# Cross-attention with a scan on one core: when x is loaded, when the scan's inputs are multiplied, and what durations the planner is given

## The chip, the cores and the metric

One core of a Trainium2 chip runs the whole kernel in one launch. The metric is device time in microseconds (us). The runs of the kernel before gave 2028.73, 2029.94 and 2029.88 us, a median of 2029.88 us.

## The reference

Everything is float32. T = 4096 tokens of width H = 512 attend with 8 heads of 64 to 3202 keys; a layer norm, a recurrent scan and an added row follow.

```python
residual = x
q_in, kv_in = layernorm(x, g1, beta1), layernorm(ctx, g1, beta1)
x = residual + mha(q_in, kv_in, W_qkv, b_qkv, W_o, b_o)      # softmax over 3202 keys
residual = x
U = (layernorm(x, g2, beta2) @ W_in.T + b_in) @ Bmat           # 64 numbers a token
s_t = silu(s_{t-1} @ A.T) + U_t                                # scan over 4096 tokens
x = residual + states @ Cmat
out = x + (ctxb.mean(axis=1) @ W_prog.T + b_prog)
```

## The kernel before

**Preparation** (the first 213 us): the context is normed, turned and multiplied into keys and values, which go to DRAM (kd, vd).

**Attention.** The 4096 tokens are eight query blocks Q of 512. A unit is one (Q, pair of heads hp, half of the block), 64 units in all, and a unit has 13 chunks of 256 keys. One chunk of one unit is a step; step number 13 x unit + chunk, 832 in all, and about 104 to a query block. A step is a matmul of scores (`scores`, s, L635), an exp on ScalarE (`weights`, p, L705), a matmul with the values four steps later (`product`, po, L745) and an addition for the softmax sum (`add`, acc, L713): VectorE does nine of a unit's twelve, GpSimd those of chunks 2, 6 and 10. At the end of a unit GpSimd folds the sum (`fold`, L720), TensorE sums it over partitions (`sums`, pd, L763), ScalarE reads it (`denominators`, L797), and VectorE adds, inverts and applies it (`whole` L801, `inverse` L804, `scale` L811, `fall` L807).

**Queries** (`queries`): while block Q is attended, x of block Q+1 is loaded in two halves of two tiles (L880), normed (`stats` L845 on VectorE, `factors` L849 to L851 on GpSimd, `scaled` xh, L857 on ScalarE), transposed in 32x32 blocks on VectorE (`flip`, L932), and moved between partitions by DMAs from SyncE's queue (`move`, L944: four pieces of four DMAs for each half). Four matmul pieces (`heads`, pq, L312) then make q. Block 7 is not flipped and moved but transposed on TensorE.

**Rows** (`project`): when block Q is done, while block Q+1 is attended, each half of its outputs is multiplied with W_o (`outs`, pa, L987, 7.1 us). x is loaded again (xr, L978), GpSimd adds a constant row (`row`, L981), VectorE adds the two (`x1`, L1000), GpSimd adds another row for the final output (`mod`, L1004), which is stored (L1007); the norm follows as for the queries, then `flip` (L932), four `move` pieces (16 DMAs, L944) and the matmul of the scan's inputs (`inputs`, pu, L1042), copied by `kept` (L1051). Tiles are named by their first token: pa_256 and pu_256 are the second half of block 0, xr_2816 the second half of block 5.

**Scan and end.** Two sweeps of 16 steps over 256 token groups follow; the last 256 tokens have a chain of their own (`last_rows`), which starts from yb (L1332).

**What sets the order.** No engine's order is written by hand. `Plan` holds pieces with an engine, a duration, the pieces they follow, a due time and rings of buffers they take and give; `order()` simulates the engines with these durations and emits the program in the order that comes out. Each engine and SyncE's queue then run in that order. A piece with the earliest due time among those ready goes first. On TensorE a piece that is not of the 64x64 kind pays 30000 ns (`ALONE`, 14 steps) on its due time unless another such piece is ready as well. `load_k` and `load_v` (L1098, L1106, ten and six steps ahead) are issued inside `scores`; the planner gives them no time on SyncE. A `move` piece is given 2600 ns there. Ring `x` has two buffers, shared by the queries' and the rows' loads; `x1` and `xn2` have one each. A due time is counted from d, the time at which a half's work begins; `from_(d)` makes a load follow a given step's scores.

Of the kernel before, what the change touches and what calls it, by code (L numbers as in the profile page):

```python
# [25 lines left out]
NDC = NCH // 2  # L26
# [22 lines left out]
STEP = 2150  # L49
# [121 lines left out]
def xattn_ssm_kernel(  # L171
# [349 lines left out]
    with tc.manual_schedule():  # L521
# [18 lines left out]
        first = shift(1)  # L540
        for c in range(NCH):
# [5 lines left out]
            parts = 1 if c < NCH - 1 else 2  # L547
            for i in range(NC // parts):
                for h in range(parts):
                    k = h * NC // parts + i  # L550
# [30 lines left out]
            for hp in range(NC):  # L581
# [9 lines left out]
                ks = cin.tile([P, GC * CK], F32, tag="ks", name=f"ks_{g}_{hp}")  # L591
# [3 lines left out]
                for b in range(g * GC, c + 1, 2):  # L595
                    m, k = blocks(b // 2) * CK, key0(b) - key0(g * GC)
# [189 lines left out]
    def finish(w, i, d, plan):  # L786

        name = w["name"]
        last = w["last"]
        ring = "s" if last else "m"  # L790

        def denominators(k):
            if k == 0:
                w["rd"] = op.tile([P, QU], F32, tag="rd", name=f"rd_{name}", bufs=2)
            of = rows_of(w, w["pd"][k][:, :QU], True)
            to = of if k else rows_of(w, w["rd"])
            nc.scalar.activation(to, of, AF.Copy, accum_out=rises[:, 3 * i + k : 3 * i + k + 1])  # L797

        def whole():
            rd = rows_of(w, w["rd"])  # L800
            nc.vector.tensor_tensor(rd, rows_of(w, w["pd"][1][:, :QU], True), rd, ALU.add)  # L801

        def inverse(part):
            nc.vector.reciprocal(w["rd"][:, part], w["rd"][:, part])  # L804

        def fall():
            nc.vector.tensor_reduce(rises[:, 3 * i + 2 : 3 * i + 3], w["rd"], AX.X, ALU.add)  # L807

        def scale(part):
            o = o_t[w["at"]][:, part]  # L810
            nc.vector.tensor_tensor(o, o, w["rd"][:, part], ALU.mult)  # L811

        plan.add(("output", i), "ACT", 360, partial(output, w), [("product", i, NDC - 1)], d, ["o_"])
        plan.add(("join", i), "DVE", 430, partial(join, w), [("output", i)], d + 500, [],
                 [("o", ("product", i, 0))])
        plan.add(("fold", i), "POOL", 1250, partial(fold, w), [("add", i, NDC - 1)], d + 500)
        plan.add(("sums", i), "PE", 450, partial(sums, w), [("fold", i)], d + 1000,
                 ["s"] if last else ["m", "m"], [("acc", ("add", i, 1))], "quarters")
        for k in range(2):
            plan.add(("den", i, k), "ACT", 420, partial(denominators, k), [("den", i, 0) if k else ("sums", i)], d + 2500 + k,  # L820
                     [] if k else ["rd"], [(ring, ("sums", i))])
        plan.add(("whole", i), "DVE", 430, whole, [("den", i, 1)], d + 3000, [], [(ring, ("sums", i))])
        parts = [slice(t * P, (t + 1) * P) for t in range(2)] if last else [slice(0, QU)]
        for t, part in enumerate(parts):
            plan.add(("inverse", i, t), "DVE", 950 if last else 1750, partial(inverse, part),
                     [("whole", i)], d + 5000 + t)
            plan.add(("scale", i, t), "DVE", 400, partial(scale, part),
                     [("inverse", i, t), ("join", i)], d + 5000 + t if last else d + 8000, [],
                     [("rd", ("den", i, 0))])
        plan.add(("fall", i), "DVE", 340, fall, [("inverse", i, t) for t in range(len(parts))],  # L830
                 d + 9000, [], [("rd", ("den", i, 0))])

    def from_(d):

        return ("scores", *divmod(min(int(d / STEP), len(steps) - 1), NDC))

    def norm_pieces(plan, ks, gets, d, after, names, gives):


        vs = [{}, {}]  # L840

        def stats_(v, get, name):
            for k, n in (("st", nc.vector.BN_STATS_DIM), ("mv", nc.vector.BN_AGGR_DIM), ("rstd", 1), ("nm", 1)):
                v[k] = ln.tile([P, n], F32, tag=f"{k}_2", name=f"{k}_{name}")
            nc.vector.bn_stats(v["st"], get())  # L845
            nc.vector.bn_aggr(v["mv"], v["st"])

        def factors_(v):
            nc.gpsimd.tensor_scalar(v["rstd"], v["mv"][:, 1:2], EPS, None, ALU.add)  # L849
            nc.gpsimd.tensor_tensor(v["rstd"], v["rstd"], neg_half, ALU.pow)  # L850
            nc.gpsimd.tensor_scalar(v["nm"], v["mv"][:, 0:1], v["rstd"], -1.0, ALU.mult, ALU.mult)  # L851

        def scaled_(v, get, t):
            if t == 0:
                for w, name in zip(vs, names):
                    w["xh"] = ln.tile([P, H], F32, tag="xh", name=f"xh_{name}")
            nc.scalar.activation(v["xh"], get(), AF.Identity, bias=v["nm"], scale=v["rstd"])  # L857

        for t, (k, v) in enumerate(zip(ks, vs)):
            plan.add((*k, "stats"), "DVE", 870, partial(stats_, v, gets[t], names[t]), [after[t]],  # L860
                     d + t, ["fs"])
            plan.add((*k, "factors"), "POOL", 1050, partial(factors_, v), [(*k, "stats")], d + 2000)
            plan.add((*k, "scaled"), "ACT", 800, partial(scaled_, v, gets[t], t),
                     [(*k, "factors")] + ([(*ks[0], "scaled")] if t else []), d + 3 * STEP + t,
                     [] if t else ["xh", "xh"], [("fs", (*k, "stats"))] + gives[t : t + 1])
        return vs

    def queries(plan, Q, d):

        copied, w = [], {}  # L870
        of_xn = ("query", Q, 0, "move0") if mixes(Q) else ("queries", Q, 0, "turn")
        for half in range(2):
            ks = [("query", Q, half * 2 + t) for t in range(2)]
            at = [Q * QB + half * QU + t * P for t in range(2)]
            k2, v = ("queries", Q, half), {}
# [5 lines left out]

            for t in range(2):
                plan.add((*ks[t], "load"), "SP", 800, partial(load, t),
                         [(*ks[0], "load")] if t else [from_(d - 2 * STEP)], d - 2 * STEP + t, [] if t else ["x"])
            free = ("x", (*ks[0], "load"))
            nv = norm_pieces(plan, ks, [lambda t=t, v=v: v["x"][:, t] for t in range(2)], d,
                             [(*k, "load") for k in ks], [f"x{r}" for r in at],
# [18 lines left out]
            after = [of_xn] if half else []  # L906
# [58 lines left out]
    def project(plan, Q, halves, d, index):  # L965

        for half in halves:
            ks = [("row", Q, half * 2 + t) for t in range(2)]
            at = [Q * QB + half * QU + t * P for t in range(2)]
            k2, vs, w = ("rows", Q, half), [{}, {}], {}  # L970
# [38 lines left out]
            units_ = [index[Q, c, half] for c in range(NC)]  # L1009
            for t in range(2):  # L1010
                plan.add((*ks[t], "load"), "SP", 800, partial(load, t),
                         [(*ks[0], "load")] if t else [from_(d - 4 * STEP)], d - 4 * STEP + t, [] if t else ["x"])
                plan.add((*ks[t], "row"), "POOL", 1300, partial(row, vs[t]), [(*ks[t], "load")], d - STEP)
            plan.add((*k2, "outs"), "PE", 7200, outs,
                     [("scale", i, 0) for i in units_] + [(*k, "row") for k in ks], d - now,
# [43 lines left out]
            if last:  # L1059
                plan.add((*k2, "turn"), "PE", 1050, turn, [(*k, "scaled") for k in ks], d + 5 * STEP - now,  # L1060
                         ["m", "m", "xn2"], [("xh", (*ks[0], "scaled"))])
                for t in range(2):
                    plan.add((*ks[t], "copy"), "ACT", 560, partial(copy, t),
                             [(*k2, "turn")] + ([(*ks[0], "copy")] if t else []), d + 6 * STEP + t, [],
                             [("m", (*k2, "turn"))])
                copied, xn2, after = [(*k, "copy") for k in ks], (*k2, "turn"), 7
            else:
                copied, xn2, after = [], (*ks[0], "move0"), 16

                def move_(a, w=w, at=at):  # L1070
                    if a == 0:
                        w["xn"] = xp_.tile([P, NC, QU], F32, tag="xn2", name=f"xn2_{at[0]}", bufs=1)
                    move(w["xn"], w["x1"], a)

                for t in range(2):
                    plan.add((*ks[t], "flip"), "DVE", 720, lambda t=t, w=w, nv=nv: flip(w["x1"], nv[t]["xh"], t),
                             [(*k, of) for k in ks for of in ("scaled", "mod")], d + 5 * STEP + t, [],
                             [("xh", (*ks[0], "scaled"))])
                for a in range(P // TB):
                    plan.add((*ks[0], f"move{a}"), "SP", 2600, partial(move_, a),  # L1080
                             [(*k, "flip") for k in ks] + ([xn2] if a else []), d + (6 + 2 * a) * STEP,
                             [] if a else ["xn2"], [("x1", (*k2, "outs"))])
                    copied.append((*ks[0], f"move{a}"))
# [392 lines left out]
    def unit(plan, i):  # L1476
# [19 lines left out]
        if half == 0:  # L1496
            d = max(s0 - REF, 0) * STEP
# [9 lines left out]
        for c in range(NDC):  # L1507
# [23 lines left out]
                         ["acc"] if c == 1 else [],  # L1531
                         [p] + ([("p", ("weights", i, 0))] if c == 1 else []))
            if c == 1:
                plan.add(("rest", i), "DVE", 700, partial(rest, w), [("add", i, 1), ("extra", first)],
                         d + 1300, [], [("extra", ("extra", first))])
        d += 2000
        finish(w, i, d - 40 * STEP if w["last"] else d, plan)
# [348 lines left out]
```

## Time and profile before

| what | value |
|---|---|
| runs, median | 2029.88 us |
| profiled execution, its own time | 2036.71 us |
| span of that execution | 2034.9 us |
| mean granted TensorE clock | 0.988 |
| TensorE matmul busy (PE) | 1967.0 us, 97% |
| VectorE (DVE) / ScalarE (ACT) / GpSimd (POOL) busy | 1210.8 / 1134.3 / 796.7 us |
| SyncE queue: moves (L944) | 416 DMAs of 32 KB |

The profile's engines are PE (matmul), PEld (weight load), DVE, ACT, POOL and SP (SyncE; its queue is SPq). Instructions issue in order on each engine, so an idle time in front of one is put down to what released it. Times inside a window are counted from the span's start.

### The profile page before, as it was taken

What the parts mean: (1) busy time and instruction counts of PE and PEld (TensorE: products, weight loads), DVE (VectorE), ACT (ScalarE), POOL (GpSimd) and SP (SyncE); (2) the same over time, 40 slices, a digit from 0 to 9 for tenths busy, and PEclk for the clock granted to TensorE, in tenths of its full rate; (3) what the DMA queues carried; (4) which work ended last, traced back from release to release, by engine and by line L of the source; (5) the groups of instructions that cost most, each with busy time, mean ns of one, the idle gap of its engine ahead of it and who ended that gap; (6) DMA issues with size and microseconds to landing.
All of it is one profiled execution on the core that took longest, in us unless ns stands there. A gap on an engine that the chain in (4) does not pass through costs nothing.

```text
span 2034.9 us, 66527 instructions
## 1 busy us (share of the span) xinstructions
PE 1967.0 (97%) x29070; PEld 1258.4 (62%) x29070; DVE 1210.8 (60%) x1533; ACT 1134.3 (56%) x1478; POOL 796.7 (39%) x631
## 2 busy tenths in 40 slices
PE   8999999999999999999999999999999999989996
PEld 4444566665666666666666566666666666655674
DVE  4321367566766666666656675677556655655585
ACT  2233566665656555555666665656565565654553
POOL 2111234345433453345334643345334533444324
PEclk9999999999999999999999999999999999999998
DMA  5632333223422343224322342233322322544475
GB/s 170 188 102 64 100 95 90 59 80 93 110 71 77 92 110 87 76 69 110 90 63 81 83 108 65 80 105 102 83 77 77 93 75 63 149 139 116 123 201 197
DMA packets 246935, 204.28 MB, mean 100 GB/s; under 512 B 80809, under 2 KB 220073, under 8 KB 246637
## 3 DMA queue, kind: packets, MB, share of 16 engines
q1 hardware_dynamic: 242088, 192.28, 33.4%
q10 hardware_dynamic: 4548, 7.67, 1.3%
q8 instruction: 231, 3.78, 0.8%
q14 instruction: 68, 0.55, 0.1%
HBM read 156.32 MB, written 29.88 MB: 92 GB/s over the span
## 4 chain that ended last, share of the span: by engine, by line
PE 70%; DVE 11%; POOL 9%; issue 3%; SPq 3%; ACT 2%; DMA 2%; DVEq 0%; POOLq 0%; ACTq 0%
PE s L635 24%; PE po L745 24%; DVE acc L713 7%; PE pq L312 5%; POOL acc L713 4%; PE pk L584 4%; PE pv L551 4%; PE pa L987 3%; SPq L944 2%; ACT p L705 1%; PE pd L763 1%; DVE rd L804 1%; DMA x<-in_x_dram 1%; POOL rstd_x L850 1%; DVE acc L699 1%
## 5 line engine op out<-in xcount | busy, mean ns | idle before, releaser
L705 ACT ACTIVATE p<-s,shifts 128x1024 f32<-128x1024 f32 (+1 forms) x832 | 889.1, 1080 | 528.5 <-PE s L635 517.4
L635 PE MATMUL s<-q,k 64*64 64x256 f32 x12800 | 839.8, 379 | 16.7 <-ACT p L705 15.6
L713 DVE TENSOR_TENSOR acc<-p,acc 128x1024 f32<-128x1024 f32 (+1 forms) x515 | 620.2, 1204 | 381.4 <-POOL acc L713 315.7
L745 PE MATMUL po<-p,v 64*64 64x256 f32 x12800 | 825.1, 378 | 0.0
L713 POOL TENSOR_TENSOR acc<-p,acc 128x1024 f32<-128x1024 f32 x189 | 446.7, 2363 | 765.4 <-DVE acc L713 419.6
L635 PEld LDWEIGHTS s<-q,k 64*64 64x64 f32 x12800 | 485.9, 134 | 248.1 <-ACT p L705 36.5
L745 PEld LDWEIGHTS po<-p,v 64*64 64x64 f32 x12800 | 491.4, 134 | 192.8 <-issue 6.1
L720 POOL TENSOR_TENSOR acc<-acc 128x512 f32<-128x512 f32 x64 | 102.1, 1595 | 141.1 <-DVE acc L713 141.1
L713 DVE TENSOR_TENSOR acc<-p,p 128x1024 f32<-128x1024 f32 x64 | 95.9, 1499 | 40.0 <-ACT p L705 34.3
L312 PE MATMUL pq<-xn,wq 128*128 128x512 f32 x256 | 118.3, 605 | 0.0
L804 DVE RECIPROCAL rd<-rd 128x256 f32<-128x256 f32 (+1 forms) x65 | 112.4, 1729 | 2.2
L987 PE MATMUL pa<-wo,o 128*128 128x512 f32 x240 | 107.0, 599 | 0.0
L551 PE MATMUL pv<-wv,ct 128*128 128x512 f32 (+1 forms) x208 | 96.4, 617 | 1.0 <-ACT ct L519 0.7
L584 PE MATMUL pk<-ct,wk 128*128 128x512 f32 (+1 forms) x224 | 88.8, 549 | 0.0
L784 DVE TENSOR_TENSOR o<-po,o 128x256 f32<-128x256 f32 x64 | 27.1, 423 | 95.3 <-ACT o L780 94.8
L312 PEld LDWEIGHTS pq<-xn,wq 128*128 128x128 f32 x256 | 46.0, 189 | 57.5 <-issue 57.5
L321 ACT ACTIVATE q<-pq,bias 128x512 f32<-128x512 f32 x32 | 22.0, 687 | 105.7 <-PE pq L312 105.7
L987 PEld LDWEIGHTS pa<-wo,o 128*128 128x128 f32 x240 | 44.4, 190 | 56.0 <-issue 56.0
L699 DVE TENSOR_TENSOR acc<-x,acc 2x256 f32<-2x256 f32 x128 | 74.9, 585 | 2.9
L519 DVE COPY ct<-tp_c 128x512 f32<-128x512 f32 (+1 forms) x13 | 8.5, 651 | 105.1 <-PE tp_c L283 105.1
L551 PEld LDWEIGHTS pv<-wv,ct 128*128 128x128 f32 (+1 forms) x208 | 38.4, 193 | 44.9 <-issue 42.7
L584 PEld LDWEIGHTS pk<-ct,wk 128*128 128x128 f32 x224 | 39.2, 190 | 42.6 <-issue 42.6
(215 smaller groups left out, 1192.8 us busy)
## 6 DMA issues: line engine op xcount, KB each, us to landing
k<-kd SPq DMA_DIRECT2D x432, 128.0 KB, 2.2
v<-vd SPq DMA_DIRECT2D x432, 128.0 KB, 2.3
xn<-x SPq DMA_DIRECT2D x416, 32.0 KB, 1.9
xr<-in_x_dram SPq DMA_DIRECT2D x30, 256.0 KB, 3.5
x1d<-xr SPq DMA_DIRECT2D x30, 256.0 KB, 2.4
x<-in_x_dram SPq DMA_DIRECT2D x28, 256.0 KB, 3.2
cx<-in_ctx_dram SPq DMA_DIRECT2D x25, 256.0 KB, 3.0
vd<-vs SPq DMA_DIRECT2D x25, 256.0 KB, 2.4
```

The source lines that it names most:

```text
L312: nc.tensor.matmul(pq, wq[:, i, hp * P : (hp + 1) * P], xn[:, i, :], start=(i == 0), stop=(i == NC - 1),)
L551: nc.tensor.matmul(pv[h * HD : h * HD + n, :H], ct[:, k, o : o + n], wv[:, k, :], start=(i == 0), stop=(i == NC // parts - 1), skip_group_ ...
L584: nc.tensor.matmul(pk[:, :n_g], wk[:, i, hp * P : (hp + 1) * P], ct[:, i, :n_g], start=(i == 0), stop=(i == NC - 1),)
L635: nc.tensor.matmul(s[k0 : k0 + HD, a, b, :], kts[(*w["at"][:2], c)][r, b * CK + k0 : b * CK + k0 + HD], q[r], start=True, stop=True, skip_ ...
L699: nc.vector.tensor_tensor(to[r], t[r], to[r], ALU.add)
L705: nc.scalar.activation(t[:, :, :nb, :], w["ps"][c][:, :, :nb, :], AF.Exp, bias=w["shift"])
L713: engine.tensor_tensor(w["acc"][:, :, :nb, :], t[:, :, :nb, :], before[:, :, :nb, :], ALU.add)
L720: nc.gpsimd.tensor_tensor(acc[:, :, 0, :], acc[:, :, 0, :], acc[:, :, 1, :], ALU.add)
L745: nc.tensor.matmul(w["po"][a * HD : (a + 1) * HD, k, :QU], vts[Q, hp, c][r, b, a * HD : (a + 1) * HD], t[r, a, b, :], start=(c == 0 and b ...
L804: nc.vector.reciprocal(w["rd"][:, part], w["rd"][:, part])
L944: nc.sync.dma_start(xn[b * TB : (b + 1) * TB, :, a * n : (a + 1) * n], of[:, b])
L987: nc.tensor.matmul(v["pa"], o_t[Q, c, half][:, t * P : (t + 1) * P], wo[:, c, :], start=(c == 0), stop=(c == NC - 1),)
```

## The change

Seven numbers change, no instruction is added or removed. Loads of x for the queries become due ten steps ahead of d (two before), loads of x for the rows twelve (four before). The scan's inputs are due 22 steps after their rows (16 before) for blocks 0 to 6. The planner is given other durations for four kinds of pieces: `fold` 1620 ns (1250), `factors` 2000 (1050), `fall` 410 (340), `rest` 1200 (700).

```diff
-        plan.add(("fold", i), "POOL", 1250, partial(fold, w), [("add", i, NDC - 1)], d + 500)
+        plan.add(("fold", i), "POOL", 1620, partial(fold, w), [("add", i, NDC - 1)], d + 500)
...
-        plan.add(("fall", i), "DVE", 340, fall, [("inverse", i, t) for t in range(len(parts))],
+        plan.add(("fall", i), "DVE", 410, fall, [("inverse", i, t) for t in range(len(parts))],
...
-            plan.add((*k, "factors"), "POOL", 1050, partial(factors_, v), [(*k, "stats")], d + 2000)
+            plan.add((*k, "factors"), "POOL", 2000, partial(factors_, v), [(*k, "stats")], d + 2000)
...
-                         [(*ks[0], "load")] if t else [from_(d - 2 * STEP)], d - 2 * STEP + t, [] if t else ["x"])
+                         [(*ks[0], "load")] if t else [from_(d - 10 * STEP)], d - 10 * STEP + t, [] if t else ["x"])
...
-                         [(*ks[0], "load")] if t else [from_(d - 4 * STEP)], d - 4 * STEP + t, [] if t else ["x"])
+                         [(*ks[0], "load")] if t else [from_(d - 12 * STEP)], d - 12 * STEP + t, [] if t else ["x"])
...
-                copied, xn2, after = [], (*ks[0], "move0"), 16
+                copied, xn2, after = [], (*ks[0], "move0"), 22
...
-                plan.add(("rest", i), "DVE", 700, partial(rest, w), [("add", i, 1), ("extra", first)],
+                plan.add(("rest", i), "DVE", 1200, partial(rest, w), [("add", i, 1), ("extra", first)],
```

## The prediction

> **What bounds the kernel now.** I read the page first.
>
> ```profile
> span 2034.9 us, 66527 instructions
> ...
> PE 1967.0 (97%) x29070; PEld 1258.4 (62%) x29070; DVE 1210.8 (60%) x1533; ACT 1134.3 (56%) x1478; POOL 796.7 (39%) x631
> ```
>
> TensorE is busy 97% of the span and the change leaves its instructions alone. So all that can be won or lost is TensorE standing still, or running at a lower clock. Second, the waits of TensorE, total, times, longest:
>
> ```profile
> PE s L635 <- ACT p L705: 15.6, 17, 2.7
> PE pd L763 <- POOL acc L720: 9.8, 4, 6.9
> ...
> PE pu L1042 <- DVE x L1000: 4.8, 1, 4.8
> PE pu L1042 <- DMA xn<-x: 4.5, 2, 3.2
> ```
>
> Few and long. The timeline places them. Five of the first kind (2.71, 2.51, 1.93, 1.73, 1.88, sum 10.8) come at 503.8, 722.7, 941.0, 1159.1 and 1377.6, once in each of the row stages of blocks 0 to 4. The first, in the timeline of all engines:
>
> ```profile
> 496.48 0.69 DVE L845 BATCH_NORM_STATS2 st_x<-x 128x6 f32<-128x512 f32 x1 [3.47 <-DMA x<-in_x_dram]
> ...
> 498.68 1.59 POOL L850 TENSOR_TENSOR rstd_x<-rstd_x,neg_half 128x1 f32<-128x1 f32 x1
> ...
> 501.34 0.81 ACT L857 ACTIVATE xh_x<-x,nm_x,rstd_x 128x512 f32<-128x512 f32 x1 [4.16 <-POOL nm_x L851]
> ...
> 503.78 1.09 PE L635 MATMUL s<-q,k 64*64 64x256 f32 x16 [2.71 <-ACT p L705]
> ```
>
> A late load of a query's x stops VectorE, GpSimd's factors take 3.8 us (497.49 to 501.31) where 1050 ns were planned, ScalarE stands in front of the norm with its exps behind it, and the scores wait for an exp. The granted clock in narrow windows shows what follows:
>
> ```profile
> 505.00:508.40 3.40, 3.40 (x40) 2.09 (x36) 2.19 (x3) 1.29 (x2) 1.26 (x2) 0.50 0.29 54
> ...
> 1641.70:1648.40 6.70, 5.95 (x56) 4.04 (x60) 2.16 (x3) 2.07 (x3) 2.35 (x1) 0.50 0.16 49
> ```
>
> The last but two column is the clock: half speed for 3.4 us after the stalls at 503.8, 722.7, 941.0 and 1887, for 6.8 us around 1642 and 1832. Half speed costs half of its time on TensorE: 1.7 us each, 3.0 and 2.0 where part lies inside the stall itself. The dips follow gaps of 1.93 us and more, none follows 1.88. The Trainium skill (TensorE: Matmul & The Clock Gate, "Why this matters for your kernels") asks for no idle gaps over some 3 us; by that the three dips of the row stages (5.1 us) would not exist and the sum below would be 5.1 us worse; the trace shows them.
>
> Third, the queue of SyncE ahead of the longest wait for moves:
>
> ```profile
> 1634.22 2.53 SPq L944 DMA_DIRECT2D xn<-x  x4
> 1636.80 0.60 SPq L1106 DMA_DIRECT2D v<-vd  x1
> 1637.44 3.20 SPq L944 DMA_DIRECT2D xn<-x  x4
> ```
>
> and TensorE's timeline there:
>
> ```profile
> 1642.45 1.98 PE L1042 MATMUL pu<-xn,wc 128*64 128x128 f32 x16 [3.16 <-DMA xn<-x]
> ```
>
> Four moves take SyncE 2.5 us, and between them stand k and v loads that the planner counts as nothing. This is the row to remember: the matmul is planned four steps behind its last move here, and the moves are 3.16 us late. In blocks 0 to 4 the distance is six steps (pu_256: move at step 159, matmul at 165), and the wait is zero four times and 1.30 us once (1426.4), with the last move landing at 551.75 for a matmul at 552.17.
>
> **The change part by part, from the built order of the changed program.** The sum is made on the profiled execution (2036.7 us; 6.8 above the median).
>
> Query loads. The second tile of x_1024 goes from step 135 to 120, its norm on ScalarE from step 141 to 125, into the 7.1 us of pa_0, where ScalarE is idle 8.38 us. So the five stalls go: 10.8 + 3 x 1.7 = 15.9 us. Left is the crowding of two more norms (2 x 0.81) before the next exps: 0.44 us wait there today, I take 0.3 more, 1.5 in all. What is late next: the x_1280 load moves from step 152 to 144 and its 16 moves from steps 160 and 161 to 148 to 151, in front of the 16 of x1_256, which stay planned at 153, 155, 157, 159.
>
> Row loads. In block 7 xr_3328 goes from step 760 to 747, xr_3584 from 785 to 775. Today GpSimd stands 11.28 and 12.49 us for these two loads, with additions, a fold and VectorE behind it, and TensorE waits 6.92 us for the fold at 1832 and 4.82 at 1887. Both go with their dips (2.0, 1.7): 15.4. In blocks 0 to 4 the second half's load (xr_256) cannot be earlier, since ring x is full: it keeps its place on the queue, ahead of GpSimd's addition; nothing is won there.
>
> Scan inputs. "22 behind" turns out not to be later. Before, pu_256 paid `ALONE`: 16 + 14 steps. Now x_1280's moves are done early, block 2's heads are ready, and no penalty is paid: it is emitted at step 163 instead of 165, four steps behind its last move, in all five second halves of blocks 0 to 4. In the first halves it goes from 141 to 143; walked the same way its moves land 1.3 us before it, so I count nothing.
>
> The price of that, for block 0. Asked: pa_256 to pu_256 takes 552.17 - 516.21 = 35.96 us, less the two steps no longer between them (4 x 0.86): 32.5 after pa. Ready: moves of x_1280 start when VectorE has flipped it, behind the additions that end 4.0 us after the start of pa today, plus two flips (1.3) and at most two statistics (1.74): 5.3 to 7.0. Then SyncE issues without a pause 32 moves x 0.64, 21 k and v loads x 0.48 and two stores x 0.48, 31.6 us, and the last lands 1.9 later: 38.8 to 40.5. The matmul waits 6.3 to 8.0 us, and everything on TensorE behind it; I take 7.5, since without the earlier stall TensorE arrives sooner while SyncE does not. The nearest row, 3.16 us, is the low end, 10 the high one. With a dip of 2.0: 5 x 9.5 = 47.5.
>
> Block 5 and after. pu_2816 keeps a wait of some 3.2 of its 6.2 us (3.16 and 3.0): two steps behind its moves, but a q matmul of 3.63 us now stands between. pu_3072 is asked for 1.7 us sooner with its moves no earlier: 1.7.
>
> Planner's durations. Better ordered folds should end the waits at 1166.8 and 1384.2 (1.62, 0.49); with the pu wait of 1.30 that is 3.4 off. `whole` and the reciprocal go ahead of the third addition of a unit, into a time when VectorE waits for GpSimd: nothing, unless pd is late, then the additions behind it are. At the end, pd_last goes behind six of the eight yb groups: 5.35 us later on TensorE. From pd to the second `scale` is 4.6 us (1973.13 to 1977.75), today hidden under 7.13 us of yb; then the last yb starts at 1983.1 instead of ending at 1980.8, of which the sweep's terms fill some: 2.5 (0 to 3.2).
>
> Removed: 15.9 + 15.4 + 6.2 + 3.4 = 40.9. Added or left: 47.5 + 3.2 + 1.7 + 1.5 + 2.5 = 56.4. Net +15.5: 2052 profiled, 2045.4 at the median of 2029.9.
>
> **Rivals.** *B, the queue catches up (faster).* SyncE waits for TensorE 583 us in all in front of k loads, so it has room; if the flips of x_1280 end early, the five waits are the 3.16 of the row at 1642, with a dip every other time (1.5): 23.5 instead of 47.5, 2021. It decides at 6.4 us a half (32.0 / 5), a wait of 4.4 with its dip: below that the change wins. Against it: these 32 moves stand back to back.
>
> *C, no wait at all.* If issuing were no bound, each move would land 1.9 us after its flip, long before step 163: all five terms vanish, 1998. The Trainium skill's "Issuing engines are not separate DMA queues" (DMA: Bandwidth & Descriptors) calls a sequencer's time to start a DMA usually small beside the DMA; here the rows say 0.6 us of issue against 1.9 to landing, and it adds up 32 times.
>
> *D, the first halves too.* If the 1.3 us of room in front of pu_0 are eaten by pauses like the one in the 3.20 row above, five more waits of 2 with a dip: +20, 2065.
>
> *E, it does nothing:* excluded by the built order, in which loads, norms, moves and pu all change places.
>
> **How the numbers follow.** Forecast 55%, B 22%, C 8%, D 15%. A measurement of this kernel tells 0.2%, 4 us, from no change. Slower: nearly all of the forecast and D, 0.65; faster: C and most of B, 0.25; the same: 0.10. The forecast's own range is 2034 to 2060; for 8 in 10 I reach down into B and leave C and most of D out: 2014 to 2060.
>
> **What would show it.** Right: no wait of s on an exp above 1 us in the row stages, GpSimd's idle on xr gone in block 7, five waits of pu on moves of 5 us and more near steps 163 + 104 n, each with half clock. Wrong: those waits under 4 us, or the 6.9 and 4.8 us waits still there.

## The result and the profile after

The changed kernel took 2088.3 us (median of 4 runs, 2084.9 to 2092.51) where the kernel before took 2029.9 (2028.73 to 2033.2): a ratio of 1.0286, with a 95% interval of 1.0262 to 1.0310. It is slower by 58.4 us where 15.5 were forecast. The profiled execution took 2089.95 us by its own time, 53.2 above the one of before.

The page of the changed kernel, span and busy times:

```profile
span 2088.2 us, 66585 instructions
...
PE 1971.2 (94%) x29070; PEld 1260.4 (60%) x29070; DVE 1190.4 (57%) x1533; ACT 1136.8 (54%) x1478; POOL 790.2 (38%) x631
```

TensorE is busy 4.2 us longer and the span is 53.3 us longer, so the time went into standing still: TensorE's gaps of over 0.25 us, added up in the trace without the first wait of the preparation (6.8 and 6.9 us), are 100.9 us where they were 50.4. Who ended them is in the waits of TensorE (total, times, longest):

```profile
PE pu L1042 <- DMA xn<-x: 58.2, 13, 9.7
PE pd L763 <- POOL acc L720: 14.5, 6, 2.9
...
PE po L745 <- DVE o L784: 6.4, 5, 4.7
PE s L635 <- ACT p L705: 3.9, 7, 0.7
...
PE yb L1332 <- DVE o L811: 2.9, 1, 2.9
```

The scores' waits for an exp fell from 15.6 to 3.9 us, as forecast, and the two long waits of block 7 are gone. In their place stands pu with 58.2 us. The timeline of SyncE's queue ahead of pu_256, and then TensorE's line:

```profile
519.84 2.53 SPq L944 DMA_DIRECT2D xn<-x  x4
...
532.14 2.54 SPq L944 DMA_DIRECT2D xn<-x  x4
...
538.28 2.83 SPq L944 DMA_DIRECT2D xn<-x  x4
...
552.29 2.53 SPq L944 DMA_DIRECT2D xn<-x  x4
```

```profile
556.20 1.98 PE L1042 MATMUL pu<-xn,wc 128*64 128x128 f32 x16 [9.05 <-DMA xn<-x]
```

Of the eight groups of four between these lines, those from 519.84 to 534.68 move x_1280, those from 538.28 on x1_256. The queue issues without a pause from 519.84 to 554.82: 32 moves of some 0.64 us, with k and v loads and two stores in between. When the last group begins, pu_256 has been standing for 5.1 us. The five second halves waited 9.05, 9.75, 9.06, 9.51 and 7.06 us: 44.4 in all.

The granted clock around this wait, from the windows of TensorE (stretch; its length, PE's busy time, its matmuls, clock, DMA share, GB/s):

```profile
548.80:552.20 3.40, 0.00 (x0) 1.00 0.42 104
552.40:559.20 6.80, 3.00 (x28) 0.50 0.34 89
```

Half clock begins inside the wait and outlasts it by 3.0 us; after the other four it lasts 5.6, 3.6, 5.8 and 3.5 us longer. Half of those 21.5 us, 10.8, is my estimate of what the dips cost here.

What the prediction had at nothing is in the timeline of all engines, in the first half of the same block:

```profile
497.30 1.06 SPq L978 DMA_DIRECT2D xr<-in_x_dram  x2
...
498.75 1.09 PE L1042 MATMUL pu<-xn,wc 128*64 128x128 f32 x16 [1.78 <-DMA xn<-x]
...
500.38 2.52 POOL L981 TENSOR_TENSOR xr<-xr,rowb 128x512 f32<-128x512 f32 x2 [8.06 <-issue]
...
502.85 2.38 POOL L713 TENSOR_TENSOR acc<-p,acc 128x1024 f32<-128x1024 f32 x1
...
505.26 2.02 DVE L713 TENSOR_TENSOR acc<-p,acc 128x1024 f32<-128x1024 f32 x2 [9.03 <-POOL acc L713]
...
507.37 2.18 POOL L720 TENSOR_TENSOR acc<-acc 128x512 f32<-128x512 f32 x1 [2.13 <-DVE acc L713]
...
509.60 0.66 PE L763 MATMUL pd<-acc,ones 64*64 64x256 f32 x8 [2.90 <-POOL acc L720]
```

pu_0 waits 1.78 us for its moves. The load of xr_256 is issued at 497.30, behind x1_0's moves; GpSimd has stood 8.06 us in front of L981, which needs it (the releaser is shown as "issue", but L981 starts 3.1 us after the load). Its addition stands behind, VectorE's addition stands 9.03 us for GpSimd's, the fold comes after both, and pd waits 2.90 us. All five blocks repeat this. x1_0's moves are late for the same kind of reason as x1_256's: in this trace two groups of x_1024's moves (471.08 and 475.66) go ahead of them on the queue, and they begin at

```profile
484.07 2.53 SPq L944 DMA_DIRECT2D xn<-x  x4
```

where in the kernel before nothing of x_1024 was ahead of them:

```profile
475.94 3.67 SPq L944 DMA_DIRECT2D xn<-x  x4
```

### The profile page after: what moved, and what is told of

It is laid out like the page before. It is cut to its first block, busy times and chain, and to the rows that moved or that the text cites. A ratio compares the mean times of both kernels' runs of the same rounds, so it can differ in the third digit from the quotient of the medians.

```text
span 2088.2 us, 66585 instructions
## 1 busy us (share of the span) xinstructions
PE 1971.2 (94%) x29070; PEld 1260.4 (60%) x29070; DVE 1190.4 (57%) x1533; ACT 1136.8 (54%) x1478; POOL 790.2 (38%) x631
## 4 chain that ended last, share of the span: by engine, by line
PE 85%; SPq 4%; issue 3%; DVE 3%; POOL 2%; DMA 1%; ACT 1%; ACTq 0%; DVEq 0%; POOLq 0%
PE s L635 30%; PE po L745 30%; PE pq L312 5%; PE pa L987 5%; PE pk L584 4%; PE pv L551 4%; SPq L944 3%; PE pd L763 1%; DVE acc L713 1%; SPq L1106 1%; PE pu L1042 1%; DMA xn<-x 1%; POOL acc L713 1%; PE sm L653 1%; PE po L733 1%
## 5 line engine op out<-in xcount | busy, mean ns | idle before, releaser
L720 POOL TENSOR_TENSOR acc<-acc 128x512 f32<-128x512 f32 x64 | 97.3, 1521 | 154.5 <-DVE acc L713 141.4
L713 DVE TENSOR_TENSOR acc<-p,p 128x1024 f32<-128x1024 f32 x64 | 87.0, 1359 | 79.7 <-ACT p L705 74.1
L1042 PE MATMUL pu<-xn,wc 128*64 128x128 f32 x240 | 21.7, 337 | 58.2 <-DMA xn<-x 58.2
L784 DVE TENSOR_TENSOR o<-po,o 128x256 f32<-128x256 f32 x64 | 26.9, 421 | 81.3 <-ACT o L780 81.0
L699 DVE TENSOR_TENSOR acc<-x,acc 2x256 f32<-2x256 f32 x128 | 69.2, 540 | 3.0
```

Source lines behind the costliest of these rows:

```text
L699: nc.vector.tensor_tensor(to[r], t[r], to[r], ALU.add)
L713: engine.tensor_tensor(w["acc"][:, :, :nb, :], t[:, :, :nb, :], before[:, :, :nb, :], ALU.add)
L720: nc.gpsimd.tensor_tensor(acc[:, :, 0, :], acc[:, :, 0, :], acc[:, :, 1, :], ALU.add)
```

## The experiments

T is the theory of the prediction: x_1280's moves stand in front of x1_256's on SyncE, and pu waits for the end of that queue. Ratios are to runs of the kernel before on the same chip; differences in us are taken from the medians, which for some pairs of runs come from different chips. Code lines are cut to the part that changes.

**1. Query loads only.**

```diff
 # kernel before
-[from_(d - 2 * STEP)], d - 2 * STEP + t
+[from_(d - 10 * STEP)], d - 10 * STEP + t      # queries
```

> The kernel before with one number changed: query loads due ten steps ahead instead of two. In its built order pu_256 is at step 163 and the 16 moves of x_1280 (steps 148 to 151) stand ahead of the 16 of x1_256, as in the changed kernel; pu_0 stays at step 141. Queue theory (the second-half waits come from these moves standing in front on SyncE): nearly all of the loss, 2089 less the block 7 gain that is missing here (plus 15) and less at most some 10 for the first halves: 2080 to 2105, with five waits of pu on moves of 8 to 10 us. Rival 'the 22 steps': the scan inputs keep their 16, so no loss: 2010 to 2035. Rival 'durations' (pieces of VectorE and GpSimd in another order make the flips late): no loss either, 2010 to 2035.

Measured: 2142.7 us, ratio 1.0553 (1.0520 to 1.0587), worse than the whole change. The second halves wait 8.8 to 9.9 us, as T says; neither rival's edit is in. But the time is 38 us above T's range. The first halves were mis-sized: pu_0 and its like wait 2.7 to 5.8 us, and the scores wait in each block for a reason the changed kernel does not have. Its timeline:

```profile
479.78 1.26 POOL L1004 TENSOR_TENSOR xr<-x,modb 128x512 f32<-128x512 f32 x1
...
481.30 1.09 PE L635 MATMUL s<-q,k 64*64 64x256 f32 x16 [1.67 <-ACT x L690]
...
483.26 0.81 ACT L857 ACTIVATE xh_y<-x,nm_y,rstd_y 128x512 f32<-128x512 f32 x1 [2.01 <-POOL nm_y L851]
...
485.12 1.13 PE L635 MATMUL s<-q,k 64*64 64x256 f32 x8 [2.73 <-ACT p L705]
```

GpSimd does mod (L1004) ahead of the second tile's norm factors, ScalarE waits 2.01 us for these, and its exps stand behind: 1.67 and 2.73 us on TensorE, with half clock behind. TensorE's busy time is 27.7 us longer than before, at a granted clock of 0.967.

**2. All but the query loads.** The changed kernel with the edit above taken back.

> The changed kernel with the query loads back at two steps. In its built order x_1280 is loaded at step 160 and moved at 161 and 172, behind x1_256's moves, and pu_256 is at step 171 (it pays the 14 steps again); but x_1024's moves (145 to 148) now stand ahead of x1_256's. Queue theory: no pu wait above 2 us in the second halves, the block 7 gain of some 15 kept, the five scores waits on an exp (10.8 us with their dips some 16) back: 2010 to 2030. Rivals '22 steps' and 'durations': both edits are still in, the loss stays: 2070 to 2090.

Measured: 2062.1 us, 1.0153 (1.0122 to 1.0184). The second-half waits are gone and the time is under both rivals' range, which falls against them, but it is 32 us above what T allowed. The first halves' waits of pu stay (1.7 to 2.7 us). x_1280 is now loaded so late that its norm stops ScalarE in front of the second half's exps: s waits 22.1 us on p, up to 3.9.

**3. Scan inputs only.**

```diff
 # kernel before
-copied, xn2, after = [], (*ks[0], "move0"), 16
+copied, xn2, after = [], (*ks[0], "move0"), 22
```

> The kernel before with the scan inputs due 22 steps behind their rows instead of 16, nothing else. Built order: pu_0 at step 143 (141), pu_256 at 169 (165), all moves where they were. Queue theory: the moves land as before and the matmul comes later, so the one wait of 1.30 us and its like go and nothing comes: 2022 to 2031. Rival '22 steps': 2060 or more.

Measured: 2033.6 us, 1.0007 (0.9993 to 1.0022): no difference in time (T's range ends at 2031), and no loss from the "22 steps" by themselves. But the trace is not the same. With pu_0 two steps later the five stalls shrink from 10.8 to 4.4 us in all, and pd, at the same place, waits 1.62, 1.63, 1.63, 2.62 and 1.64 us for the fold, where before it waited in two blocks only (1.62 and 0.49). The first of them:

```profile
509.67 0.66 PE L763 MATMUL pd<-acc,ones 64*64 64x256 f32 x8 [1.62 <-POOL acc L720]
```

What the stalls give up, the fold takes.

**4. Durations only.**

> The kernel before with the four planner durations of the changed kernel (fold 1620, factors 2000, fall 410, rest 1200), nothing else. Built order: pa_256 at 148 (149), pu_0 and pu_256 at 141 and 165 as before, x_1280's moves at 161. Queue theory: no new wait of pu; scores waits on an exp may move by a few us: 2015 to 2035. Rival 'durations': the additions behind fold and whole are late, waits of pd on a fold of 2 to 3 us come up in each block and the time is 2050 or more.

Measured: 2053.3 us, 1.0109 (1.0079 to 1.0139): 22 us slower, T's range missed, and the time is the one of the rival 'durations' (2050 or more), though not by its wait: pd does not wait for a fold in each block but for VectorE's x1 (L1000), 11.2 us in ten waits. No new wait of pu came of it. The durations pushed x_1280's load from step 152 to 159:

```profile
546.02 0.69 DVE L845 BATCH_NORM_STATS2 st_x<-x 128x6 f32<-128x512 f32 x1 [7.37 <-DMA x<-in_x_dram]
...
550.16 1.15 PE L635 MATMUL s<-q,k 64*64 64x256 f32 x12 [4.16 <-ACT p L705]
```

VectorE stands 7.37 us for x, the norm on ScalarE comes after that, and the scores stand 4.16 us for an exp behind it. A late x load stopped the scores in both places; it is the mechanism of the five stalls before, at another step.

**5. The same queue, pu six steps later.**

```diff
 # changed kernel
-plan.add((*k2, "inputs"), "PE", 700, inputs, copied, d + after
+plan.add((*k2, "inputs"), "PE", 700, inputs,
+    copied + ([from_(d + 34 * STEP)] if half and not last else []), d + after
```

> The changed kernel in which the second half's matmul of the scan's inputs (blocks 0 to 6) must also follow the scores 34 steps behind d: built order has pu_256 at step 169 instead of 163, SyncE's queue is instruction for instruction that of the changed kernel. Queue theory: the moves land when they land, and a matmul asked for six steps of 1.72 us later (10.3 us) finds them there; the five second-half waits of 7.1 to 9.8 us (44 in all) go, the first-half waits (1.3 to 1.9) and those of pd on fold (2.6 to 2.9) stay: 2036 to 2050. Rival 'rate': SyncE issues too many DMAs a block in any case, so that the moves slip along with the matmul: waits of 4 us and more stay and the time is 2060 or more.

**6. x_1280's moves behind x1_256's.**

```diff
 # changed kernel, queries
-after = [of_xn] if half else []
+after = [of_xn] + [("row", Q - 2, 2, "move3")] * (1 < Q < NQB - 1) if half else []
```

> The changed kernel in which the moves of a query block's second half must follow the fourth move of the rows' second half (x_1280 behind x1_256): loads of x as early as in the changed kernel, built order has x_1280's moves from step 160 and pu_256 at 169. Queue theory: x1_256's moves land early, no second-half wait over 2 us; first-half and fold waits stay: 2036 to 2050, as with the later matmul. Rival 'VectorE': the flips of x1_256 themselves come late because of the earlier norms, the waits stay at 5 us or more: 2065 to 2090.

Measured: 5 took 2046.3 us, 1.0072 (1.0054 to 1.0090); 6 took 2037.4, 1.0017 (1.0001 to 1.0033). The waits of pu in 5, then in 6:

```profile
PE pu L1042 <- DMA xn<-x: 22.5, 13, 3.4
```

```profile
PE pu L1042 <- DMA xn<-x: 13.2, 8, 3.1
```

These two settle the loss. With SyncE's queue untouched and only the matmul later, 42 us come back against the changed kernel; with the matmul at the same late step and the queue turned round, 51. In 6 no second half of blocks 0 to 4 waits over 0.4 us. In 5 they still wait 0.7 to 2.0: in block 0 pu_256 is asked for 10.1 us later (557.2 against 547.1), as reckoned, but its moves land 3.1 us later as well (559.3 against 556.2). 1.0 of this is the stage's own later start (pa_256 at 516.19 against 515.16); the rest is lost along the queue, for a cause that was not found. The "rate" rival can hold for that part, no more.

**7 and 11. Early row loads alone, in the last blocks.**

```diff
 # kernel before; run 7: last, run 11: Q > 5
-[from_(d - 4 * STEP)], d - 4 * STEP + t
+[from_(d - (12 if Q > 5 else 4) * STEP)], d - (12 if Q > 5 else 4) * STEP + t
```

> The kernel before with one change: in block 7 alone the rows' loads are due twelve steps ahead. The 6.92 and 4.82 us waits and their dips (15.4 together, by the prediction's working) should go and nothing else move: 2014 to 2020. If the waits only hid other late work, less than 8 us is won: 2022 to 2030.

> The kernel before with the rows' loads of blocks 6 and 7 due twelve steps ahead. The run with block 7 alone moved only the load of xr_3584 (waited 4.82 us before) and took 6.9 us off; xr_3328 belongs to the rows of block 6, and the 6.23 us wait of pd on the fold was still there. With both: 15.4 off by the prediction's working, 2014 to 2020. If the fold was late for another reason: 2024 to 2028, with that wait still there.

Measured: 7 took 2025.7 us, 0.9973 (0.9962 to 0.9984); 11 took 2023.0, 0.9941 (0.9920 to 0.9962). Run 7 was laid out wrong: xr_3328 is loaded in block 7 but belongs to the rows of block 6, so one of the two waits stayed, and the expected 2014 to 2020 was missed. Its timeline:

```profile
1825.69 1.13 PE L763 MATMUL pd<-acc,ones 64*64 64x256 f32 x8 [6.23 <-POOL acc L720]
```

The 6.9 us won match the 4.82 and the dip (1.7) of xr_3584's load. In run 11 both waits are gone, but 11.4 us are won instead of 15.4 (2023.0, again above 2014 to 2020), for pu_3072 now comes too soon for its moves:

```profile
1808.74 1.97 PE L1042 MATMUL pu<-xn,wc 128*64 128x128 f32 x16 [3.92 <-DMA xn<-x]
```

**8. Row loads only, in all blocks.**

> The kernel before with the rows' loads due twelve steps ahead in all blocks. Built order: xr_256 takes the free buffer at step 122, before x_1024's load, which goes to 135; x_1280's goes to 160, its moves to 161 and 171; pu_0 at 138 (141), pu_256 at 165. From the runs so far, all but the query loads is 31 slower, of which durations alone are 22 and the scan inputs nothing: 2037 to 2042, with waits of scores on an exp of some 2 to 4 us in blocks 0 to 4. Rival: the durations made all of that, and the block 7 gain stands: 2010 to 2022.

Measured: 2062.1 us, 1.0136 (1.0113 to 1.0159), 20 us above what adding up the runs gave. xr_256 takes the free buffer of ring x first, x_1280 comes at step 160, and the scores wait 3.6 to 4.7 us for its norm in each of blocks 0 to 4 (33.4 us on p in all). Each of the two early loads alone is slow; effects of such edits do not add.

**9. Behind, and the row addition behind the softmax addition.** Run 6 with one more dependency:

```diff
-[(*ks[t], "load")], d - STEP)                                # row, L981
+[(*ks[t], "load")] + ([("add", 8 * Q + 10, 10)] if half and Q < 6 else []), d - STEP)
```

> The kernel of the run 'x1280 moves behind' (2037) with one more dependency: in the second halves of blocks 0 to 5 GpSimd's row addition (L981) must follow its third softmax addition of that unit. Built order: L713 of chunk 10 stands ahead of both L981 of xr_256, pu_0 at step 146 instead of 143, pu_256 at 169. Theory (the waits of pd on a fold come from GpSimd standing some 8 us in front of L981 for xr_256, with the addition and the fold queued behind): the five waits of 2.6 to 3.0 (13.7 in all) and the join's 0.42 behind each (2.1) go, the first-half pu waits of 1.3 to 2.3 (8.2 in all) go with the later step: 2011 to 2020, which would be faster than the kernel before. Rival: the chain through the fold is late for VectorE's or ScalarE's own sake: the waits stay, 2030 to 2040; or the later row addition makes pa_256 wait as much as is won: 2030 to 2040 with a wait of pa or of x1 in place of them.

Measured: 2013.2 us (2012.3 to 2020.37), 0.9901 (0.9872 to 0.9931): faster than both kernels. Its timeline at the place of the long idle time above:

```profile
496.08 2.37 POOL L713 TENSOR_TENSOR acc<-p,acc 128x1024 f32<-128x1024 f32 x1 [4.06 <-DVE acc L713]
...
498.49 2.91 DVE L713 TENSOR_TENSOR acc<-p,acc 128x1024 f32<-128x1024 f32 x2 [2.55 <-POOL acc L713]
...
499.30 3.23 POOL L981 TENSOR_TENSOR xr<-xr,rowb 128x512 f32<-128x512 f32 x2 [0.84 <-POOL acc L713]
...
504.79 0.76 PE L763 MATMUL pd<-acc,ones 64*64 64x256 f32 x8 [0.23 <-POOL acc L720]
```

The third addition goes first, L981 waits for nothing but it, VectorE waits 2.55 us instead of 9.03, pu not at all and pd 0.23 (0.2 to 1.1 in the five blocks). The first halves' waits (pu, pd and the join of VectorE, L784, behind pd) fall from 24.0 us in run 6 to 4.3; the profiled executions of the two lie 18.1 us apart, the medians 24. pu_0 is three steps later here too, so the share of that and of GpSimd's order were not told apart.

**10. The same without durations.** Run 9 with the old durations and the first half's pu held to step 146.

> As the run before it, but with the planner's durations of the kernel before, and the first-half scan inputs held to the same step 146. Theory that the durations matter only where they order GpSimd's pieces in the row stages (in 'query loads only', with the old durations, mod L1004 stands ahead of the norm's factors and the scores wait 1.7 and 2.7 us an half): those waits are here, 4.4 us and a dip in each of blocks 0 to 4, against 3 us saved at the end of the kernel (the wait of yb): some 20 to 30 above the run before it. Rival 'durations cost 22', as alone: 10 to 25 below it.

Measured: 2042.5 us, 1.0035 (1.0018 to 1.0052), 29 above run 9, with 0.5 and 2.7 us of waiting scores in each row stage (1.7 and 2.7 in run 1, and expected here).

**12. All but the durations.**

> The changed kernel with the planner's four durations of the kernel before. Built order: pu_256 at 163, x_1280's moves at 148 to 151 as in the changed kernel. If the 54 us between 'query loads only' (2143) and the changed kernel come from the durations (factors ahead of mod): 2120 to 2140. If they come from the rows' loads: 2080 to 2095. If durations simply cost what they cost alone (22): 2062 to 2070.

Measured: 2136.9 us, 1.0495 (1.0454 to 1.0537), in the range of the first of the three theories. Against the changed kernel the durations are worth 42 us by the ratios to before and 49 by the medians; alone they cost 22.

## Why the prediction was wrong, step by step

The side was right, and so was the cause of most of the loss; the size was not. Steps of the sum against the profiled execution, in us:

| step of the prediction | forecast | measured |
|---|---|---|
| stalls of the row stages, blocks 0 to 4 | 15.9 off, 1.5 left | gone; waits of 0.68 a block left |
| first halves, pu and what follows | 0 | 8.2 pu + 14.0 pd + 1.7 join |
| second halves, pu and dips | 47.5 | 44.4 + 10.8 |
| pu_2816 and block 5 | 3.2 | 1.6 + 4.7 + 0.6 |
| pu_3072 | 1.7 | 3.4 |
| tail | 2.5 | 2.9 |
| block 7's two waits | 15.4 off | gone |

The errors are 23.9, 7.7, 3.7, 1.7 and 0.4, 37.4 together; with the 15.5 forecast 52.9, against 53.2 measured. That it comes out so near is partly luck: half clock behind four more waits (1430.37, 1687.66, 1870.97 and 2029.11; some 10 us by the rule of half) is not in the table, and TensorE's busy time, in which all half clock shows, is only 4.2 us longer than before.

**The step that failed is the first halves' zero.** "its moves land 1.3 us before it, so I count nothing" was walked on the trace of before, in which TensorE loses 2.7 us and a dip in that very stretch. I took the stall out of the sum but left the time at which TensorE arrives as it was. And "What is late next" was answered with the x_1280 load alone. GpSimd's chain (L981 for xr_256, addition, fold, pd) was on show in the kernel before:

```profile
501.27 2.49 POOL L981 TENSOR_TENSOR xr<-xr,rowb 128x512 f32<-128x512 f32 x2
503.72 2.35 POOL L713 TENSOR_TENSOR acc<-p,acc 128x1024 f32<-128x1024 f32 x1
508.21 2.19 POOL L720 TENSOR_TENSOR acc<-acc 128x512 f32<-128x512 f32 x1 [2.13 <-DVE acc L713]
```

pd ran at 511.35 without a wait, since the stall had delayed TensorE. In blocks 3 and 4, with the shortest stalls, pd already waited (1.62 and 0.49 us), and the prediction took these waits off its sum; in the changed kernel they are 2.79 and 2.91. In its block 0 the fold starts 0.8 us earlier than before (507.37), but TensorE asks for pd 4.6 us earlier (506.70). Run 3 shows the cover at work: shorter stalls, longer waits of pd, the same time. So the 15.9 us did not turn into time: 23.9 came up in their place.

Nor did the chain's start stay where it was. In the kernel before GpSimd came to L981 behind the factors of the late x (497.49 to 501.31), when the load of xr_256, issued at 494.05, had landed (498.17). In the changed kernel these factors are out of the way, but the load is issued at 497.30, since x1_0's moves in front of it are later, and L981 stands for it until 500.38. "it keeps its place on the queue" was right, and "nothing is won there" too; that the place itself comes 3.3 us later was not seen. This part is read from the traces; no run moved that load alone. Rival D named the first halves, with pu's waits alone; it gave 2065.

**Second halves.** The mechanism held to the step: 163, 32 moves back to back, 9 us instead of 7.5. In block 0 TensorE asks 32.0 us after pa's start (32.5 forecast) and x_1280's moves begin 4.7 after it (5.3 to 7.0 forecast); the term that was too small is the queue's issue time, 35.0 us (519.84 to 554.82) instead of 31.6. 2.0 for a dip was right (10.8 / 5 = 2.2). Rival B, that the queue catches up, is out, and so is C: issue at 0.64 us a move was the bound, 20 us over 32 moves. The Trainium skill (DMA: Bandwidth & Descriptors, "Issuing engines are not separate DMA queues") calls the sequencer's time to start a DMA usually small beside the DMA; here it is 0.64 us against 1.9 from issue to landing, and it adds up.

**Block 5.** Not foreseen: x for block 7's queries is loaded at 1680.77 behind xr's, and its norm holds up VectorE's join:

```profile
1684.67 0.69 DVE L845 BATCH_NORM_STATS2 st_x<-x 128x6 f32<-128x512 f32 x1 [6.71 <-DMA x<-in_x_dram]
...
1687.22 0.39 DVE L784 TENSOR_TENSOR o<-po,o 128x256 f32<-128x256 f32 x1
1687.66 1.98 PE L745 MATMUL po<-p,v 64*64 64x256 f32 x16 [4.69 <-DVE o L784]
```

**Durations.** Taken to end the two waits for the fold (2.1 of the 3.4 us), which grew instead, and otherwise to be worth nothing. Runs 10 and 12 show them to be the edit that keeps the factors ahead of mod once the loads are early; without them the change costs 102 us, not 58. Which of the four does it was not told apart. I had looked at their effect on fold and whole only, in the full change, and never asked what the loads would do without them; the forecast's sum did not need that, as both were in.

**Block 7 and the tail** went as forecast, pu_3072's wait excepted, which is twice its term.

In run 6 pu_0 and its like still wait 1.3 to 2.3 us: their moves are not behind x_1280's, but half of x_1024's are still ahead of them, as in the changed kernel (x1_0's begin at 484.15). Left open: whether turning that order round as well would end these waits without the later step of run 9, and what a third buffer in ring x would do; neither was tried.

## What to carry to other kernels

Before a stall is taken out of the sum, walk every chain that ends in the same stretch as if the stall were gone: what is on time only because the consumer is late is the next wait, and it may cost more. An earlier load moves everything that hangs on it, here 16 DMAs of half a query block, to a new place on an in-order queue; count that queue by its issue time, and if it is full, order the urgent transfers first (run 6) instead of moving the consumer (run 5). Edits to a planner's numbers do not add up: the durations cost 22 us alone and save over 40 beside the early loads, so test each with the others in and with the others out.

## What the runs showed of the hardware

The prediction read from one trace that half clock follows gaps of 1.93 us and more. Over all 14 traces, between 430 and 1950 us, half clock ran during a gap of TensorE or began within 4 us of its end for 60 of 62 gaps of 3 us and more, 38 of 62 gaps of 2 to 3 us, and 11 of 74 gaps of 1 to 2 us. The two exceptions are gaps of 3.19 us (run 10) and 3.39 us (run 5). In the changed kernel four of the five waits of pd of 2.6 to 2.9 us have none. The Trainium skill (TensorE: Matmul & The Clock Gate, "Why this matters for your kernels") asks for no idle gaps over some 3 us. Above 3 the traces agree with these two exceptions; between 2 and 3 us more than half of the gaps had a dip all the same.
